# A second MLP product from seven quarter products, with work moved between VectorE, ScalarE and GpSimd around it

## The chip, the cores and the metric

The kernel runs on one core of one Trainium2 chip, in one launch. The metric is the device time in microseconds, as the median of several executions. An engine-by-engine profile of one execution stands beside it. The engines go by these names: PE is TensorE (PEld is its loading of stationary operands), DVE is VectorE, ACT is ScalarE, POOL is GpSimd, and SP is the engine that issues most of the DMAs.

## The reference

The input x has the shape (4, 64, 512, 64). Everything is float32. The output has 4 × 4096 tokens of width 256. Cut to what matters:

```
h = rfft_patches(x) @ W.T                        # tokens of width 256
y = layernorm(h)                                 # z of the kernel
r = y + retention(layernorm(y))                  # q * scan(decay, k * v)
a = relu(layernorm(r) @ W1.T + b1)               # 256 -> 1024
h = h + r + a @ W2.T + b2                        # 1024 -> 256, "second MLP product"
t = layernorm(h)                                 # tok of the kernel
h = h + t + sum over the two best experts e of weight_e * (gelu(t @ w1[e] + b1[e]) @ w2[e] + b2[e])
```

## The kernel before

The 16384 tokens are worked on in 32 blocks of 512 tokens (four tiles of 128). The loop over blocks is a software pipeline: in one iteration `new` (block i) is embedded, normed and sent through retention, `mid` (block i−1) goes through the MLP, and `old` (block i−2) is routed to its experts. Beside that, tiles of 256 tokens that already wait in a buffer in device memory (`xbuf`, sorted by expert) go through their expert in "slots" (`slot`, which calls `expert_step`), four in an iteration once the pipeline is full. The loop has 31 iterations; the work of the last block, and what is then left of the two before it, is written out by hand behind it.

The order of work on SP, PE, DVE and ACT is the order in which the program issues it (`manual_schedule`); each of these engines works strictly down its list. GpSimd is not in that list: its order is chosen by the framework's scheduler, from what is ready and from the order in the program. Within one iteration the order is this:

1. `embed` (L337 to L386): ten products of `xv` and `wu` on PE (L353; forty instructions), which DVE adds up into `h` (L359, L379); two norm factors by GpSimd (`factors`, L243 to L248); DVE then writes `zz`, the norm of the norm, and `z`, the first norm's result (L252 in `Norm.apply`). Between the first two parts `features2` of mid joins the turned halves to `hT` on ACT, and `rows`, `turn3` and `store` of old are issued. Ahead of the last part comes `sum_up` of mid (L462, L463): h + z + b2 on DVE.
2. A slot. Then eight `mlp_in(m)` of mid: a product on PE (L298) and a ReLU on ACT (L482), which frees a PSUM buffer; there are four such buffers (`p_mm`). After m = 1 stands `split1`: from block 6 on, two ACT copies (L278, `planes`) and a DMA that turns them; in blocks 0 to 5 PE turns `zz` instead. After m = 3 stands a slot. After m = 5 come `differences` of the next block (nine DVE instructions, L327 and L330) and `features1`, which joins the turned halves to `hT` on DVE (L292).
3. `logits` of old on PE (L557), `retention(0)` and `retention(1)` of new (three products each; ACT L416; DVE L418, L426, L436), with `choose` of old (sixteen small DVE instructions, L579 to L595) between them. `place` (PE L624, DVE L626 to L635) gives every row its place in `xbuf`; `take` (L702 to L744) works out a table of the tiles that have become full, in small DVE instructions on one partition. GpSimd writes the rows into `xbuf` by eight indirect DMAs (`scatter`, L647).
4. A slot, `mlp_out(0)`, `residual` (PE L451, DVE L454; then `factors_here` on DVE and `zz`), a slot, `split2`, the loads of the next tiles, and `mlp_out(1)`.

`mlp_out(u)` multiplies two tiles of 128 tokens, 8 × 2 products of 128 × 128 with 128 × 256 (L492; every float32 product is two instructions), and adds them to `h` (L499). After the second call come the norm statistics, the factor on GpSimd, `tok` (L252 again) and `by`.

A slot issues, in this order: the load of a tile (`load`: weights `w`, transposing read `xh`, and `xg`, all on SP, with the table's values read into registers), `turn` (ACT L806), `enter` (PE L813, ACT gelu L821), `leave` (PE L830), and `sums` (DVE L842 to L849, then two indirect DMAs of GpSimd that add into the output, L853).

Of the kernel before, what the change touches and what calls it, by code (L numbers as in the profile page):

```python
# [19 lines left out]
P = 128  # L20
# [15 lines left out]
def vit_tower_kernel(  # L36
# [21 lines left out]
    KD, KH = D // P, H // P  # L58
    J = STRIDE // 2
# [90 lines left out]
    w2_sb = const.tile([P, KH, D], F32)  # L150
    nc.sync.dma_start(out=w2_sb, in_=w2.rearrange("(k p) d -> p k d", p=P))
# [14 lines left out]
    nc.gpsimd.iota(tile_f, pattern=[[1, KMAX]], base=0, channel_multiplier=0, allow_small_or_imprecise_dtypes=True)  # L166
    ones_e = const.tile([1, E], F32)
# [24 lines left out]
    six = ctx.enter_context(tc.tile_pool(name="six", bufs=6))  # L192
# [116 lines left out]
    class Block:  # L309
# [5 lines left out]
        def differences(self, xb):  # L315
# [22 lines left out]
            more(v[0], v[0], 2.0, v[3])  # L338
            less(v[4], s0[:, :, 1:], s2)
            more(v[4], v[3], -2.0, v[4])  # L340

        def embed(self):
# [40 lines left out]
            self.z = one.tile([P, TT, D], F32, name="z")  # L383
            self.zz = one.tile([P, TT, D], F32, name="zz")
            norm.apply(self.zz, self.h, 1)
            norm.apply(self.z, self.h, 0)  # L386
# [74 lines left out]
        def sum_up(self):  # L461
            nc.vector.tensor_tensor(self.h, self.h, self.z, ALU.add)  # L462
            nc.vector.tensor_tensor(self.h, self.h, mb2_sb.unsqueeze(1).to_broadcast([P, TT, D]), ALU.add)  # L463
# [19 lines left out]

        def mlp_out(self, u, between=None):
            if u == 0:
                self.norm = Norm()
            ps = p_tm.tile([P, 2, D], F32, name="tm")
            for i in range(2):
                if i and between:
                    between()  # L490
                for k in range(KH):
                    last_product[0] = nc.tensor.matmul(  # L492
                        ps[:, i, :],
                        lhsT=self.aT[:, k, ts(u * 2 + i, P)],
                        rhs=w2_sb[:, k, :],
                        start=k == 0,
                        stop=k == KH - 1,
                    )
            nc.vector.tensor_tensor(self.h[:, ts(u, 2), :], ps, self.h[:, ts(u, 2), :], ALU.add)  # L499
            for i in range(2):  # L500
                self.norm.stats(self.h, u * 2 + i)
            if u == U - 1:
                self.norm.factors_here() if self.i >= NS - 1 else self.norm.factors()
                self.tok = one.tile([P, TT, D], F32, name="tok")
                self.norm.apply(self.tok, self.h)
                if self.i == NS:
                    nc.vector.tensor_tensor(self.h, self.h, self.tok, ALU.add)
                    return
                mean, rstd = self.norm.mv[:, :, 0], self.norm.rstd[:, 0, :]
                self.by = small.tile([P, 2, TT], F32, name="by")  # L510
                nc.vector.tensor_scalar(self.by[:, 0, :], rstd, 1.0, None, ALU.add)
                nc.vector.scalar_tensor_tensor(self.by[:, 1, :], mean, -1.0, rstd, ALU.mult, ALU.mult)
# [52 lines left out]
        def choose(self):  # L565
# [7 lines left out]
            lg = small.tile(shape, F32, name="lg")  # L573
# [8 lines left out]
            key = small.tile(shape, F32, name="key")  # L582
            self.oh = oh = small.tile([P, 2, TT, E], F32, name="oh")
# [35 lines left out]
        def place(self, at_once=True):  # L619
# [5 lines left out]
            before = small.tile([P, TT, E], F32, name="before")  # L625
# [70 lines left out]
    def take(n, block, writes):  # L696
# [17 lines left out]

# [24 lines left out]
        if block.i >= NS - 1:  # L739
            nc.vector.tensor_scalar(table[:, 2, :], table_f[:, 0, :], float(E - 1), None, ALU.min)  # L740
# [9 lines left out]
    def load_bank():  # L750
# [4 lines left out]
        for e in range(E):  # L755
            nc.scalar.dma_start(out=bank[0][:, e, :], in_=wex[ts(e, P), :])
            loaded.append(e)
            yield

    AHEAD = 4  # L760
    last_product = [None]
    tiles = []
    added = []
# [448 lines left out]
```

## Time and profile before

| What | Value |
|---|---|
| Median of 3 runs (lowest to highest) | 2172.19 us (2169.8 to 2180.58) |
| Profiled execution | 2177.78 us, span 2176.0 us |
| PE busy | 2149.1 us, 99% |
| DVE busy | 1648.2 us, 76% |
| ACT busy | 831.3 us, 38% |
| POOL busy | 874.5 us, 40% |
| Second MLP product (L492) on PE | 453.5 us, 2048 instructions |
| Mean granted PE clock | 0.993 |

A group's row in the profile reads: line, engine, operation, what is written from what, shapes, count; then the time in which the group was busy and the mean length of one instruction in ns; then the time that the engine idled just before the group, and on what. PE's instructions overlap, so the mean length is longer than the time from one start to the next. A line of the timeline reads: start in us, length, engine, line, operation, operands, count of merged instructions, and in brackets the idle time before and what ended it. Lengths on POOL are rough.

### The profile page before, as it was taken

The page shows a single profiled execution, that of the slowest core. Times are in us where ns is not written, and L with a number is a line of the kernel's source. Part 1 is how long each engine was busy: PE and PEld are TensorE (multiplying, and loading weights), DVE is VectorE, ACT ScalarE, POOL GpSimd, SP SyncE. Part 2 cuts the span into 40 slices and gives each one's busy share as a digit, 9 for nine tenths or more (in the row PEclk, how much of TensorE's full clock was granted, in tenths as well). Part 3 has the DMA queues.
Part 4 walks back from the last instruction along what each step waited for, and adds up shares of the span by engine and source line. Part 5 has one row for each costly group of instructions (what it writes and reads, how often), then busy time and mean ns, then how long its engine had stood idle before and what let it go on. Part 6 is the DMA issues. An engine that isn't in the chain of part 4 may idle for free.

```text
span 2176.0 us, 28966 instructions
## 1 busy us (share of the span) xinstructions
PE 2149.1 (99%) x8548; PEld 1546.0 (71%) x8548; DVE 1648.2 (76%) x5150; ACT 831.3 (38%) x1329; POOL 874.5 (40%) x760
## 2 busy tenths in 40 slices
PE   8999999999999999999999999999999999998999
PEld 6666666677776667777666777666777766676776
DVE  6678877778778778777877877877787887766454
ACT  1222333444334444433444443344343334442543
POOL 1022233444443344444334444433444443355444
PEclk9999999999999999999999999999999999999999
DMA  3032255765666776565677655576755666788743
GB/s 137 20 98 76 76 129 127 161 146 127 136 127 148 151 161 142 132 134 128 148 151 161 141 133 123 130 150 152 166 121 131 137 133 152 135 166 219 118 67 46
DMA packets 425390, 284.96 MB, mean 131 GB/s; under 512 B 355216, under 2 KB 391056, under 8 KB 421136
## 3 DMA queue, kind: packets, MB, share of 16 engines
q1 hardware_dynamic: 374304, 210.21, 42.0%
q0 software_dynamic: 49632, 67.39, 17.3%
q10 hardware_dynamic: 1296, 5.52, 0.9%
q8 instruction: 67, 1.10, 0.2%
q14 instruction: 91, 0.75, 0.1%
HBM read 118.36 MB, written 88.39 MB: 95 GB/s over the span
## 4 chain that ended last, share of the span: by engine, by line
PE 93%; DVE 3%; DMA 2%; issue 1%; another core or an unknown queue 0%; ACT 0%; DVEq 0%; SPq 0%
PE mm L298 33%; PE tm L492 19%; PE tm L353 13%; PE mm L813 10%; PE tm L830 10%; DMA turned<-planes 2%; PE sm L557 2%; PE tm L905 1%; PE mm L888 1%; PE tm L451 1%; PE mm L131 1%; PE mm L265 1%; PE sm L624 0%; DVE ks L426 0%; PE sm L204 0%
## 5 line engine op out<-in xcount | busy, mean ns | idle before, releaser
L853 POOL DMA_INDIRECT out<-y,xg x262 | 428.2, 1634 | 468.5 <-DVE y L849 210.2
L298 PE MATMUL mm<-hT,w_sb 128*128 128x512 f32 x1024 | 452.1, 594 | 4.3 <-issue 4.3
L492 PE MATMUL tm<-w_sb,aT 128*128 128x256 f32 x2048 | 453.5, 379 | 1.7 <-DVE h L499 1.7
L492 PEld LDWEIGHTS tm<-w_sb,aT 128*128 128x128 f32 x2048 | 388.6, 190 | 55.8 <-DVE h L499 2.1
L298 PEld LDWEIGHTS mm<-hT,w_sb 128*128 128x128 f32 x1024 | 194.6, 191 | 222.1 <-issue 213.2
L647 POOL DMA_INDIRECT xbuf<-row,to x248 | 243.7, 983 | 259.1 <-DVE full L708 182.6
L298 PE MATMUL mm<-hT,wqkv_sb 128*128 128x512 f32 x768 | 342.5, 602 | 2.3 <-DVE hT L292 2.2
L353 PE MATMUL tm<-wu,xv 128*128 128x256 f32 x1280 | 284.8, 381 | 0.0
L298 PEld LDWEIGHTS mm<-hT,wqkv_sb 128*128 128x128 f32 x768 | 145.2, 192 | 174.6 <-issue 159.0
L353 PEld LDWEIGHTS tm<-wu,xv 128*128 128x128 f32 x1280 | 244.2, 191 | 33.3
L821 ACT ACTIVATE ge<-mm,w 128x256 f32<-128x256 f32 x262 | 109.2, 468 | 405.7 <-issue 356.0
L813 PE MATMUL mm<-xT,w 128*128 128x256 f32 x1048 | 250.8, 382 | 0.0
L482 ACT ACTIVATE aT<-mm,vec 128x512 f32<-128x512 f32 x256 | 172.6, 684 | 204.7 <-PE mm L298 202.7
L830 PE MATMUL tm<-w,ge 128*128 128x256 f32 x1048 | 248.8, 380 | 0.9 <-DVE y L847 0.9
L830 PEld LDWEIGHTS tm<-w,ge 128*128 128x128 f32 x1048 | 200.0, 191 | 31.8 <-issue 3.4
L813 PEld LDWEIGHTS mm<-xT,w 128*128 128x128 f32 x1048 | 194.8, 190 | 37.0 <-issue 14.1
L806 ACT COPY xT<-xh 128x512 uint16<-128x512 uint16 x262 | 181.3, 762 | 11.3 <-DMA xh<-xbuf 6.3
L243 POOL TENSOR_SCALAR rstd<-mv 128x4 f32<-128x4 f32 x62 | 41.6, 672 | 317.2 <-DVE mv L224 315.3
L278 ACT COPY planes<-zz 128x1024 uint16<-128x1024 uint16 x100 | 99.6, 1043 | 163.9 <-issue 101.5
L847 DVE TENSOR_TENSOR y<-tm,w 128x512 f32<-128x512 f32 x131 | 90.6, 692 | 69.0 <-PE tm L830 65.2
L416 ACT ACTIVATE ks<-mm,vec 128x512 f32<-128x512 f32 x64 | 44.0, 687 | 243.2 <-PE mm L298 243.2
L597 POOL TENSOR_TENSOR ex<-euler,second 128x4 f32<-128x4 f32 x32 | 34.5, 1079 | 240.7 <-DVE second L589 240.7
(155 smaller groups left out, 2445.2 us busy)
## 6 DMA issues: line engine op xcount, KB each, us to landing
w<-in_wex SPq DMA_DIRECT2D x113, 641.5 KB
xb<-in_x SPq DMA_DIRECT2D x32, 1040.0 KB
out<-h SPq DMA_DIRECT2D x31, 512.0 KB
bank<-in_wex ACTq DMA_DIRECT2D x8, 641.5 KB
out<-y,xg POOLq DMA_INDIRECT x262
xbuf<-row,to POOLq DMA_INDIRECT x248
xh<-xbuf SPq DMA_TRANSPOSE x131
xg<-xbuf SPq DMA_DIRECT2D x131, 4.0 KB
```

The source lines that it names most:

```text
L278: nc.scalar.copy(planes[:, :, i * D : (i + 1) * D], half)
L298: nc.tensor.matmul(ps, lhsT=w[:, k, ts(m, P)], rhs=rhs[:, k, :], start=k == 0, stop=k == KD - 1)
L353: nc.tensor.matmul(ps[:, n, :], lhsT=xv[:, i, j, :], rhs=wu[:, i, j, :], start=j == 0, stop=j == J - 1)
L482: nc.scalar.activation(self.aT[:, m, :], ps, AF.Relu, bias=vec[:, MB1 + m : MB1 + m + 1])
L492: last_product[0] = nc.tensor.matmul(ps[:, i, :], lhsT=self.aT[:, k, ts(u * 2 + i, P)], rhs=w2_sb[:, k, :], start=k == 0, stop=k == KH - 1,)
L647: write = nc.gpsimd.indirect_dma_start(out=xbuf, out_offset=bass.IndirectOffsetOnAxis(ap=self.to[:, c, t : t + 1], axis=0), in_=self.row[: ...
L806: nc.scalar.copy(halves[:, :, :, 1 - i], self.xh[:, i * KD : (i + 1) * KD, :])
L813: nc.tensor.matmul(ps[:, m, :], lhsT=self.w[:, k * D + m * P : k * D + (m + 1) * P], rhs=self.xT[:, k, :], start=k == 0, stop=k == KD - 1,)
L821: nc.scalar.activation(self.ge[:, m, :], ps[:, m, :], AF.Gelu, bias=self.w[:, 5 * D + m : 5 * D + m + 1])
L830: last_product[0] = nc.tensor.matmul(ps[:, c, :], lhsT=self.ge[:, k, ts(c, P)], rhs=w[:, (2 + k) * D : (3 + k) * D], start=k == 0, stop=k ...
L847: nc.vector.tensor_tensor(y, ps, w[:, 4 * D : 5 * D].unsqueeze(1).to_broadcast([P, 2, D]), ALU.add)
L853: add = nc.gpsimd.indirect_dma_start(out=out, out_offset=bass.IndirectOffsetOnAxis(ap=self.xg[:, c, NUMBER - D : NUMBER - D + 1], axis=0), ...
```

## The change

The second MLP product is written as a product of 2 × 2 blocks by Strassen's method (in Winograd's form). The left operand, the 512 × 1024 activations, and the right one, 1024 × 256 weights, are cut into quarters; seven products of quarters replace the eight. The weight combinations are made once (`combine_weights`), those of the activations in each block on DVE (`combine1`, `combine2`), and the products are added into `h` by DVE; `mlp_out` now has three calls (16, 32 and 64 instructions of width 128).

Beside it, work moves. `sum_up` goes from DVE to GpSimd, and is issued later. The first norm's `z` goes from DVE to ACT (`result1`). `take`'s second half goes from DVE to GpSimd, up to block 27, in simpler instructions. `differences` is split in two. The slot ahead of `mlp_in` no longer issues a load; the load comes after `split1`, whose transposes so stand ahead of it on SP; `store` comes after m = 4. `xh` has four buffers in place of six, and some small tiles one in place of two. S1, S2 and S4 use the buffers of `tok`, `tokT` and `kv`. The diff, cut:

```diff
-    w2_sb = const.tile([P, KH, D], F32)
-    nc.sync.dma_start(out=w2_sb, in_=w2.rearrange("(k p) d -> p k d", p=P))
+    w2_sb = const.tile([P, 7, KQ, P], F32)
+    w2_raw = w2.rearrange("(r k p) (c d) -> p r c k d", p=P, k=KQ, d=P)
+    for i, (r, c) in {B11: (0, 0), B21: (1, 0), B22: (1, 1), T1: (0, 1)}.items():
+        nc.sync.dma_start(out=w2_sb[:, i], in_=w2_raw[:, r, c])
+    def combine_weights():
+        nc.vector.tensor_tensor(w2_sb[:, T3], w2_sb[:, B22], w2_sb[:, T1], ALU.subtract)
+        nc.vector.tensor_tensor(w2_sb[:, T1], w2_sb[:, T1], w2_sb[:, B11], ALU.subtract)
+        nc.vector.tensor_tensor(w2_sb[:, T2], w2_sb[:, B22], w2_sb[:, T1], ALU.subtract)
+        nc.vector.tensor_tensor(w2_sb[:, T4], w2_sb[:, B21], w2_sb[:, T2], ALU.subtract)
...
-            self.z = one.tile([P, TT, D], F32, name="z")
...
-            norm.apply(self.z, self.h, 0)
+            self.norm1 = norm
+        def result1(self):
+            mean, rstd = self.norm1.mv[:, :, 0], self.norm1.rstd[:, 0, :]
+            less = small.tile([P, TT], F32, name="less")
+            self.z = one.tile([P, TT, D], F32, name="z")
+            nc.vector.scalar_tensor_tensor(less, mean, -1.0, rstd, ALU.mult, ALU.mult)
+            for t in range(TT):
+                nc.scalar.activation(
+                    self.z[:, t, :],
+                    self.h[:, t, :],
...
-        def sum_up(self):
...
+        def sum_up(self, engine=nc.gpsimd):
+            engine.tensor_tensor(self.h, self.h, self.z, ALU.add)
+            engine.tensor_tensor(self.h, self.h, mb2_sb.unsqueeze(1).to_broadcast([P, TT, D]), ALU.add)
...
+        def combine1(self):
+            self.A11, self.A12 = [self.aT[:, i * KQ : (i + 1) * KQ, : BLK // 2] for i in range(2)]
+            self.A21, self.A22 = [self.aT[:, i * KQ : (i + 1) * KQ, BLK // 2 :] for i in range(2)]
+            shape = [P, KQ, BLK // 2]
+            self.S1 = one.tile(shape, F32, name="tok")
+            self.S2 = one.tile(shape, F32, name="tokT")
+            self.S3 = self.A21
+            nc.vector.tensor_tensor(self.S1, self.A21, self.A22, ALU.add)
+            nc.vector.tensor_tensor(self.S2, self.S1, self.A11, ALU.subtract)
+            nc.vector.tensor_tensor(self.S3, self.A11, self.A21, ALU.subtract)
+        def combine2(self, place):
+            self.S4 = one.tile([P, KQ, BLK // 2], F32, name=place)
+            nc.vector.tensor_tensor(self.S4, self.A12, self.S2, ALU.subtract)
         def mlp_out(self, u, between=None):
+            def product(to, a, b):
+                for i in range(2):
+                    for k in range(KQ):
+                        last_product[0] = nc.tensor.matmul(
+                            to[:, i, :],
+                            lhsT=a[:, k, ts(i, P)],
+                            rhs=w2_sb[:, b, k, :],
...
+            def add(to, what):
+                nc.vector.tensor_tensor(to, to, what, ALU.add)
+            h = self.h.rearrange("p (a i) (c d) -> p a c i d", i=2, d=P)
+            U = self.aT[:, 0, : BLK // 2].rearrange("p (i d) -> p i d", d=P)
             if u == 0:
...
+                self.ps = p_sm.tile([P, 2, 2, P], F32, name="sm")
+                product(self.ps[:, 0], self.A11, B11)
+                nc.scalar.copy(U, self.ps[:, 0])
+                add(h[:, 0, 0], U)
+                return
+            if u == 1:
+                ps = p_tm.tile([P, 2, 2, P], F32, name="tm")
+                product(ps[:, 0], self.A12, B21)
...
+                product(ps[:, 1], self.A22, T4)
+                add(h[:, :, 0], ps)
+                return
+            product(self.ps[:, 1], self.S2, T2)
+            product(self.ps[:, 0], self.S1, T1)
+            add(U, self.ps[:, 1])
+            add(h[:, 0, 1], U)
+            add(h[:, :, 1], self.ps[:, 0].unsqueeze(1).to_broadcast([P, 2, 2, P]))
...
+            product(ps[:, 0], self.S3, T3)
+            product(ps[:, 1], self.S4, B22)
+            add(U, ps[:, 0])
+            add(h[:, 1], U.unsqueeze(1).to_broadcast([P, 2, 2, P]))
+            add(h[:, 0, 1], ps[:, 1])
+            self.norm = Norm()
+            for t in (2, 3, 0, 1):
+                self.norm.stats(self.h, t)
...
+        engine = nc.vector if block.i >= SOON else nc.gpsimd
...
+    SOON = NS - 3
...
-            self.xh = six.tile([P, 2 * KD, S], U16, name="xh")
+            self.xh = four.tile([P, 2 * KD, S], U16, name="xh")
...
-    def slot(known):
+    def slot(known, load=True):
...
-                old.store()
             next(embed)
             next(embed)
-            if mid:
-                mid.sum_up()
+            if i + 1 < NB:
+                blocks[i + 1].differences(xs.pop(i + 1), 0)
             next(embed, None)
-            slot(known)
+            slot(known, load=False)
...
                     new.split1()
+                    if at["enter"]:
+                        advance("load", at["enter"] + AHEAD - 1)
                 if m == TT - 1:
                     slot(known)
+                if m == KH // 2 and old:
+                    old.store()
                 if m == KH - 3:
-                    blocks[i + 1].differences(xs.pop(i + 1))
+                    blocks[i + 1].differences(None, 1)
                     new.features1()
+                    if mid:
+                        mid.sum_up()
...
+            if mid:
+                mid.combine1()
             for m in range(KD):
                 new.retention(m)
+                if m == 0:
+                    new.result1()
                 if old and m == 0:
                     old.choose()
...
             slot(known)
+            if mid:
+                mid.mlp_out(0)
             if old:
                 old.scatter(2, last_product[0])
             if mid:
-                mid.mlp_out(0)
+                mid.combine2("kv")
+                mid.mlp_out(1)
             if old:
                 old.scatter(3, last_product[0])
             new.residual()
-            slot(known)
+            slot(known, load=False)
...
             if mid:
-                mid.mlp_out(1)
+                mid.mlp_out(2)
```

In `take`, the instructions from `base` (L716) to `taken` (L744) go to `engine`. The two sums over experts (L730, L732), which reduced along the row, become halving adds, and instructions with three operands become two, so that fourteen instructions become seventeen.

## The prediction

> **What bounds the kernel now.** I read the page first, then TensorE's timeline of one steady block (number 15 of 32, 1005 to 1069 us), then the same stretch of GpSimd, VectorE and ScalarE, then the waits.
>
> From the page:
>
> ```profile
> PE 2149.1 (99%) x8548; PEld 1546.0 (71%) x8548; DVE 1648.2 (76%) x5150; ACT 831.3 (38%) x1329; POOL 874.5 (40%) x760
> L492 PE MATMUL tm<-w_sb,aT 128*128 128x256 f32 x2048 | 453.5, 379 | 1.7 <-DVE h L499 1.7
> ```
>
> TensorE never rests, and the product that changes (L492) takes 453.5 us of it, with 1.7 us of waiting. Timeline of TensorE (start, length, count):
>
> ```profile
> 1009.68 7.07 PE L492 MATMUL tm<-w_sb,aT 128*128 128x256 f32 x32
> 1016.59 1.04 PE L451 MATMUL tm<-ident,ret 128*128 128x128 f32 x8
> ...
> 1020.92 7.07 PE L492 MATMUL tm<-w_sb,aT 128*128 128x256 f32 x32
> 1027.82 8.80 PE L353 MATMUL tm<-wu,xv 128*128 128x256 f32 x40
> ...
> 1050.23 7.03 PE L298 MATMUL mm<-hT,w_sb 128*128 128x512 f32 x16
> 1057.10 1.85 PE L557 MATMUL sm<-rw_sb,tokT 128*128 128x8 f32 x16
> 1058.80 10.55 PE L298 MATMUL mm<-hT,wqkv_sb 128*128 128x512 f32 x24
> ```
>
> Work follows work without a gap, so a stall anywhere lengthens the block. A 256-wide instruction takes 6.91/32 = 216 ns from start to start. GpSimd in the same block:
>
> ```profile
> 1011.60 1.06 POOL L647 DMA_INDIRECT xbuf<-row,to  x1 [6.46 <-DVE full L708]
> ...
> 1024.39 0.96 POOL L647 DMA_INDIRECT xbuf<-row,to  x1 [0.30 <-issue]
> 1028.04 1.61 POOL L853 DMA_INDIRECT out<-y,xg  x1 [2.69 <-DVE y L849]
> 1029.95 1.57 POOL L853 DMA_INDIRECT out<-y,xg  x1 [0.30 <-DVE mv L224]
> 1031.59 0.23 POOL L243 TENSOR_SCALAR rstd<-mv 128x4 f32<-128x4 f32 x1
> 1031.91 1.04 POOL L248 TENSOR_TENSOR rstd<-rstd,mhalf 128x4 f32<-128x4 f32 x1
> ...
> 1039.65 1.11 POOL L243 TENSOR_SCALAR rstd<-mv 128x4 f32<-128x4 f32 x1 [6.58 <-DVE mv L224]
> ```
>
> GpSimd is only 40% busy, but from 1011.6 on it is a queue: eight scatters (1.28 us apart), four scatter-adds (1.9 apart), and behind them the norm's factor (L243, L248), for which VectorE waits. VectorE and ScalarE after it, and the wait in total:
>
> ```profile
> 1032.99 1.38 DVE L252 TENSOR_SCALAR tok<-h,mv,rstd 128x256 f32<-128x256 f32 x4 [3.06 <-POOL rstd L248]
> 1039.48 1.19 DVE L462 TENSOR_TENSOR h<-h,z 128x1024 f32<-128x1024 f32 x1
> ...
> 1043.77 1.38 DVE L252 TENSOR_SCALAR zz<-h,mv,rstd 128x256 f32<-128x256 f32 x4 [1.84 <-POOL rstd L248]
> ```
>
> ```profile
> 1045.24 1.99 ACT L278 COPY planes<-zz 128x1024 uint16<-128x1024 uint16 x2 [1.01 <-DVE zz L252]
> 1047.14 1.26 ACT L482 ACTIVATE aT<-mm,vec 128x512 f32<-128x512 f32 x2
> ```
>
> ```profile
> DVE tok L252 <- POOL rstd L248: 81.2, 30, 3.1
> ```
>
> This is the chain that TensorE would meet next: factor, tok, VectorE's work on the new embedding, zz, planes, and behind planes the ReLUs that free PSUM.
>
> [...] the 8-wide logits (L557), each with a load, take (1058.80 − 1057.10)/16 = 106 ns, and single ones start 112 ns apart. [...] L243 took 0.23 us with VectorE idle and 1.11 beside L462. [...]
>
> **The change, part by part, per block.**
>
> *Products.* Out: 64 instructions at 216 ns = 13.8 us. In: 7 products × 2 × 4 × 2 passes = 112 of width 128. Their multiplying alone would be half of 216, 108 ns (the 128-wide transposes, L451, do 8 in 0.87 us, 109 each), so the load's 112 decides: 12.5. Gain 1.3 us × 32 = 41. Bounds: at 106 ns 1.9 per block (62 us); if loads did not overlap, 190 ns (L492's own load row on the weight-load engine), 21.3 us and 240 lost; the logits exclude that. I take 41.
>
> *VectorE.* In: four combinations of 1024 elements at 1.2 (L462) = 4.8; five adds of 256 at 0.4 and three of 512 at 0.69 (L499) = 4.1 in place of 1.4; one small factor 0.2. Out: residual sums 2.4 (L462, L463), first norm's z 1.4, fourteen instructions of the table (L716 to L744, 1011.85 to 1014.3) 2.45. Net +1.4, or 45 us on 1648: not a bound by sum. The three first combinations lie between the last ReLU (1058.0) and the first value product (1062.6, where VectorE idles 3.4 us): 3.6 fits into 4.6, cost nothing; without that cover, up to 3.6. The small factor stands ahead of choose, whose result the placing product awaits with 0.4 to spare: 0.2 × 29 = 5 us.
>
> *ScalarE.* z costs 2.07 (as L518) and a copy of 256 some 0.4: +80 us on 831, covered by the 4.5 us in which it waits for L298; without it, 2 us on the next ks.
>
> *Transfers.* split1's transposes were issued at 1051.23 though planes ended at 1047.23, because the queue held a tile's load (1046.76 to 1050.63). Now the load's three DMAs and two register loads come after them, and a store of 512 KB after mlp_in 4. That is up to 4 us for hT, which gates retention at 1058.80. Loads run three tiles ahead, so theirs cost nothing; nor do four xh buffers and the single ones, freed a step or a block earlier.
>
> *GpSimd.* Seventeen table instructions per block, chained. Each at least 0.32 us (L243 to L248), at most 0.67 (L243's mean, waits included): 5.4 to 11.4; I take 0.38[...]: 6.5. In program order they stand ahead of scatter, scatter-adds and factor. Two residual sums: [...] at least VectorE's 1.2. They are ready once z is, and behind what stands earlier.
>
> *Where that goes.* Let E be the end of the second product, 1027.8 before and 1026.5 after. Before, tok starts at E + 5.2. After: GpSimd's queue 1011.6 + 17.8 + 6.5 = 1035.9, factor 1.4: 1037.3, E + 10.8. VectorE is ready earlier: three last adds 1.5 and four statistics at 0.6, E + 4.1. How late may tok be? zz followed tok's start by 10.8 + 1.3 = 12.1 before; after, six difference instructions at 0.6 replace sums and idling, about the same. Planes take 2.0, the third ReLU 0.7, latencies 0.3; TensorE needs that PSUM buffer at its sixth mlp_in, 1050.23 + 1.72 = E + 24.1. So zz by E + 21.1, tok by E + 9.0. (hT's way, zz + 2.1 + 5.5 for the transpose, 1028.46 to 1034.01, + 1.5 to E + 31.0, allows 0.8 more.) Late by 1.8. The residual sums follow the factor on GpSimd, just where VectorE wants two-input adds on the embedding; held 0 to 2.8 us, I take 1.0. Stall: 2.8 us per block.
>
> It holds only from block 6 on, where zz is turned by planes: 25 blocks, 70 us. Sum: −41 + 70 + 5, and 2 to 3 in the tail, where TensorE has one expert step (3.45) over four combinations (4.8) and the longer last adds: +37. The profiled execution took 2177.8 (span 2176.0), 0.3% over the median 2172.2; so 2215 against it, **2209** against the median. At start, three more issues (about 1 us each) and four weight combinations (2.8) lie in block 0, where VectorE waits.
>
> **Rivals.**
> *A, faster.* GpSimd absorbs it: table instructions near 0.32, sums in its idle stretch (1059.3 to 1067.5), tok in time. Then −41 + 5 + 3: **2139**. It decides where the stall is below 33/25 = 1.3 us, that is, added GpSimd time ahead of tok plus VectorE's hold below 6.1 (I have 7.5). For it: the margin is thin, and 40% busy leaves room. Against: that queue already ran 1.7 us behind the statistics.
> *B, much slower.* The scheduler, which orders GpSimd by readiness, puts the sums ahead of the factor: 4.4 more, stall 6.2, 155 us: 2172 − 41 + 155 + 8 = **2294**. For it: z is ready some 10 us before the factor. Against: the queue still holds earlier work then.
> *C, slower elsewhere.* The sums run near 1059, beside the combinations: VectorE held up to 4.4, 1.0 of it covered, so about 2.5 on kv, choose and the placing product: −41 + 29 × 2.5 + 8: **2211**.
>
> **How the numbers follow.** Forecast 0.35 (own range 2183 to 2245), A 0.32 (2125 to 2161), C 0.13, B 0.12, all but cancelling 0.08. The forecast and C give one time by one cause, GpSimd's new work holding VectorE, and carry it over A. Within 0.5% (2161 to 2183; a measurement can hardly tell less from no change) falls 0.10; below 0.32; above 0.58. Below 2130 lies 0.06 of A, above 2265 most of B: range 2130 to 2265.
>
> **What would show it.** Right: width-128 products start 112 ns apart; VectorE's wait at tok grows from 2.7 us each to 7 or more; TensorE shows gaps of 2 to 3 us at mlp_in or retention. A: the wait at tok stays under 6 and TensorE shows none. B: the two sums stand ahead of L243's successor. C: gaps at the placing product. The forecast is wrong if the table's instructions take under 0.3 us, if scatters overlap them, or if loads and 128-wide products interfere (over 112 ns, slower whatever GpSimd does).

## The result and the profile after

The changed kernel takes **2275.41 us** (median of 4 runs, 2274.43 to 2277.9) against 2173.43 us for the kernel before in the same comparison. The ratio is 1.0467, with a 95% interval of [1.0438, 1.0496]. The forecast was 2209, in a range of 2130 to 2265: the sign was right, but the loss is 102 us and not 37.

The profiled execution took 2276.34 us, with a span of 2274.6 us. Its busy times, and the rows of the new product and of the MLP's first product (columns as in the profile before):

```profile
PE 2139.8 (94%) x10084; PEld 1560.7 (69%) x10084; DVE 1781.5 (78%) x4949; ACT 895.0 (39%) x1489; POOL 1140.1 (50%) x1280
...
L543 PE MATMUL tm<-w_sb,aT 128*128 128x128 f32 x1536 | 184.2, 277 | 0.0
...
L312 PE MATMUL mm<-hT,w_sb 128*128 128x512 f32 x1024 | 470.4, 604 | 91.6 <-ACT ge L912 44.4 <-ACT aT L518 43.0 <-issue 4.0
```

PE is busy for 9 us less than before, but it is busy for only 94% of the span. The product is as fast as forecast: its instructions start 112 ns apart, so that it takes 12.5 us of a block where it took 13.8. The loss is in another product, `mlp_in` (L312): 91.6 us of waiting, half on the gelu of an expert tile (`ge`), half on the third ReLU (`aT`). One steady block in PE's timeline:

```profile
1018.52 8.80 PE L375 MATMUL tm<-wu,xv 128*128 128x256 f32 x40
...
1030.61 5.31 PE L312 MATMUL mm<-hT,w_sb 128*128 128x512 f32 x12
1037.65 1.98 PE L312 MATMUL mm<-hT,w_sb 128*128 128x512 f32 x4 [1.73 <-ACT ge L912]
...
1046.63 5.42 PE L312 MATMUL mm<-hT,w_sb 128*128 128x512 f32 x12 [1.83 <-ACT aT L518]
```

The second product ends at 1018.5, which is the E of the prediction. The fourth `mlp_in` starts 1.7 us late and the sixth 1.8. GpSimd in the same block shows why, and VectorE and ScalarE show what hangs on it:

```profile
1018.42 0.97 POOL L731 DMA_INDIRECT xbuf<-row,to  x1 [0.30 <-issue]
1019.41 2.36 POOL L498 TENSOR_TENSOR h<-h,z 128x1024 f32<-128x1024 f32 x1
1021.85 2.70 POOL L499 TENSOR_TENSOR h<-h,mb_sb 128x1024 f32<-128x1024 f32 x1
1024.70 0.99 POOL L731 DMA_INDIRECT xbuf<-row,to  x1 [0.15 <-issue]
...
1030.82 0.23 POOL L257 TENSOR_SCALAR rstd<-mv 128x4 f32<-128x4 f32 x1
```

```profile
1019.17 3.16 DVE L552 TENSOR_TENSOR h<-h,aT 128x512 f32<-128x512 f32 x1
1022.25 0.41 DVE L552 TENSOR_TENSOR h<-h,tm 128x256 f32<-128x256 f32 x1
1022.58 0.41 DVE L237 BATCH_NORM_STATS2 st<-h 128x6 f32<-128x256 f32 x1
...
1024.61 0.18 DVE L238 BATCH_NORM_AGGREGATE mv<-st 128x2 f32<-128x6 f32 x1
1032.21 1.38 DVE L266 TENSOR_SCALAR tok<-h,mv,rstd 128x256 f32<-128x256 f32 x4 [7.41 <-POOL rstd L262]
```

```profile
1033.63 1.99 ACT L617 COPY row<-tok 128x1024 uint16<-128x1024 uint16 x2 [6.45 <-DVE tok L266]
1035.53 1.38 ACT L897 COPY xT<-xh 128x512 uint16<-128x512 uint16 x2
1036.77 0.82 ACT L912 ACTIVATE ge<-mm,w 128x256 f32<-128x256 f32 x2
...
1044.00 1.99 ACT L292 COPY planes<-zz 128x1024 uint16<-128x1024 uint16 x2 [5.25 <-DVE zz L266]
1045.90 1.26 ACT L518 ACTIVATE aT<-mm,vec 128x512 f32<-128x512 f32 x2
```

The two residual sums (L498, L499) stand between two scatters, ahead of the norm's factor (L257). tok so starts at E + 13.7 (1032.21 − 1018.52), where it was E + 5.2 before. ScalarE, which works down its list, is held at `row` (which reads tok), so the gelu that frees a PSUM buffer is late; 10 us later it is held at `planes` (which read zz), so the third ReLU is late. VectorE does lose time beside the first sum: an addition (L552) takes 3.16 us instead of 0.69. But that is not what makes tok late here. Its last addition and the norm statistics run beside the second sum at their usual lengths, and the last statistic ends at 1024.79, 6.0 us before the factor starts; in blocks 7 to 30 that distance is 6.0 to 6.1 us throughout. In the changed kernel it is the place of the sums in GpSimd's queue that counts. In the whole run VectorE's wait at tok grew from 81.2 to 192.9 us:

```profile
DVE tok L266 <- POOL rstd L262: 192.9, 30, 7.4
```

The second loss is in the first blocks. I measure a block from its first embedding product to the next block's. Against the profiled execution of before, blocks 0 to 5 are 21.9 us longer in sum, blocks 6 to 30 are 73.7 us longer (2.9 each), and the last one with the tail is 2.5 us longer. In blocks 2 to 4 the new first product waits for its PSUM bank (`sm`), which VectorE still reads for `place`:

```profile
212.03 3.63 PE L543 MATMUL sm<-w_sb,aT 128*128 128x128 f32 x16 [3.47 <-DVE before L714]
```

It waits 3.5 us, and then its sixteen instructions take 3.6 us instead of 1.95, since they start some 213 ns apart: the granted clock is 0.5 from 212.2 to 215.6 us.

### The profile page after: what moved, and what is told of

The parts are those of the page before. It is cut to its first block, busy times and chain, and to the rows that moved or that the text cites. A ratio compares the mean times of both kernels' runs of the same rounds, so it can differ in the third digit from the quotient of the medians.

```text
span 2274.6 us, 32705 instructions
## 1 busy us (share of the span) xinstructions
PE 2139.8 (94%) x10084; PEld 1560.7 (69%) x10084; DVE 1781.5 (78%) x4949; ACT 895.0 (39%) x1489; POOL 1140.1 (50%) x1280
## 4 chain that ended last, share of the span: by engine, by line
PE 45%; DVE 25%; POOL 15%; issue 8%; ACT 4%; DMA 2%; SPq 1%; POOLq 0%; ACTq 0%; DVEq 0%
PE mm L312 21%; POOL xbuf L731 5%; PE tm L543 5%; POOL out L944 5%; PE mm L904 4%; DVE st L237 3%; PE tm L921 3%; PE sm L543 3%; POOL h L498 3%; PE sm L641 2%; DVE h L381 2%; DVE xv L348 2%; DVE zz L266 2%; PE tm L375 2%; DVE mv L238 2%
## 5 line engine op out<-in xcount | busy, mean ns | idle before, releaser
L944 POOL DMA_INDIRECT out<-y,xg x262 | 441.4, 1685 | 355.7 <-DVE y L940 133.3
L312 PE MATMUL mm<-hT,w_sb 128*128 128x512 f32 x1024 | 470.4, 604 | 91.6 <-ACT ge L912 44.4
L312 PEld LDWEIGHTS mm<-hT,w_sb 128*128 128x128 f32 x1024 | 191.4, 192 | 329.7 <-issue 188.0
L731 POOL DMA_INDIRECT xbuf<-row,to x248 | 253.3, 1021 | 252.9 <-DVE full L792 184.2
L312 PE MATMUL mm<-hT,wqkv_sb 128*128 128x512 f32 x768 | 338.4, 597 | 1.5 <-DVE hT L306 1.5
L312 PEld LDWEIGHTS mm<-hT,wqkv_sb 128*128 128x128 f32 x768 | 143.8, 191 | 170.7 <-issue 155.3
L266 DVE TENSOR_SCALAR tok<-h,mv,rstd 128x256 f32<-128x256 f32 x128 | 44.2, 409 | 193.0 <-POOL rstd L262 192.9
L897 ACT COPY xT<-xh 128x512 uint16<-128x512 uint16 x262 | 181.3, 760 | 10.6 <-DMA xh<-xbuf 10.6
L543 PE MATMUL tm<-w_sb,aT 128*128 128x128 f32 x1536 | 184.2, 277 | 0.0
L518 ACT ACTIVATE aT<-mm,vec 128x512 f32<-128x512 f32 x256 | 164.6, 689 | 44.1 <-PE mm L312 44.1
L543 PEld LDWEIGHTS tm<-w_sb,aT 128*128 128x128 f32 x1536 | 179.2, 194 | 0.1
L257 POOL TENSOR_SCALAR rstd<-mv 128x4 f32<-128x4 f32 x62 | 25.9, 417 | 265.2 <-DVE mv L238 263.4
L617 ACT COPY row<-tok 128x1024 uint16<-128x1024 uint16 x62 | 61.7, 1043 | 212.8 <-DVE tok L266 212.8
L416 ACT ACTIVATE z<-h,less,rstd 128x256 f32<-128x256 f32 x128 | 66.4, 588 | 150.4 <-DVE lg L663 132.4
```

Source lines behind the costliest of these rows:

```text
L266: nc.vector.tensor_scalar(dst[:, t, :D], src[:, t, :], self.mv[:, t, 0:1], self.rstd[:, i, t : t + 1], ALU.subtract, ALU.mult,)
L312: nc.tensor.matmul(ps, lhsT=w[:, k, ts(m, P)], rhs=rhs[:, k, :], start=k == 0, stop=k == KD - 1)
L518: nc.scalar.activation(self.aT[:, m, :], ps, AF.Relu, bias=vec[:, MB1 + m : MB1 + m + 1])
L543: last_product[0] = nc.tensor.matmul(to[:, i, :], lhsT=a[:, k, ts(i, P)], rhs=w2_sb[:, b, k, :], start=k == 0, stop=k == KQ - 1,)
L731: write = nc.gpsimd.indirect_dma_start(out=xbuf, out_offset=bass.IndirectOffsetOnAxis(ap=self.to[:, c, t : t + 1], axis=0), in_=self.row[: ...
L897: nc.scalar.copy(halves[:, :, :, 1 - i], self.xh[:, i * KD : (i + 1) * KD, :])
```

## The experiments

My theory after the result: the two sums on GpSimd cost on both sides. They lengthen the queue ahead of tok's factor by 5.1 us, and while they run they hold VectorE's instructions up. The rivals: that the queue alone counts (the table's seventeen instructions included), or that the seven products themselves are too much for VectorE. The table gives all runs: the median, the ratio to the kernel before measured beside it, and the lengths of the blocks against the profiled execution of before, added up as above.

| Run | Median, us | Ratio, 95% interval | Blocks 0–5 | Blocks 6–30 | Block 31 |
|---|---|---|---|---|---|
| changed kernel | 2275.41 | 1.0467 [1.0438, 1.0496] | +21.9 | +73.7 | +2.5 |
| a1: sums on VectorE | 2210.69 | 1.0167 [1.0144, 1.0190] | +12.8 | +15.0 | +4.6 |
| a2: table on VectorE | 2283.43 | 1.0496 [1.0467, 1.0524] | +27.4 | +77.0 | +3.1 |
| a3: sums behind the factor | 2280.40 | 1.0485 [1.0461, 1.0508] | +27.4 | +71.1 | +2.9 |
| a4: first products swapped | 2295.60 | 1.0556 [1.0521, 1.0591] | +12.1 | +101.9 | +3.5 |
| a5: tok's factor on VectorE | 2224.97 | 1.0246 [1.0226, 1.0265] | +23.5 | +12.6 | +3.0 |
| b1: sums on VectorE, ahead of the join | 2162.50 | 0.9957 [0.9942, 0.9971] | +10.2 | −30.0 | +3.1 |
| b2: seven products alone | 2227.31 | 1.0248 [1.0228, 1.0269] | +14.5 | +29.0 | +5.6 |
| b3: sums on GpSimd, in the kernel before | 2317.90 | 1.0662 [1.0637, 1.0688] | +11.8 | +130.2 | +3.7 |
| c1: b1 with its first blocks mended | 2148.02 | 0.9892 [0.9872, 0.9912] | −1.5 | −28.8 | +9.2 |
| c2: b1, table on VectorE | 2172.09 | 1.0008 [0.9994, 1.0022] | +2.1 | −9.6 | +0.7 |
| c3: b1, z on VectorE | 2198.14 | 1.0116 [1.0087, 1.0144] | +12.1 | +14.4 | +2.7 |
| c4: b1, transfers put back | 2205.46 | 1.0147 [1.0121, 1.0172] | +9.4 | +30.3 | +2.0 |

### The sums: on GpSimd or not, and where in its queue

**a1_sums_dve**, the changed kernel with the sums on VectorE, at the same place behind the join of `hT`:

```diff
-                        mid.sum_up()
+                        mid.sum_up(nc.vector)
```

> The kernel after, with the two residual sums back on VectorE at the place where the program issues them (behind the join of hT). Queue theory (what GpSimd does ahead of tok's factor sets tok, and tok sets the waits at mlp_in): 5.1 us leave GpSimd's queue, the wait at tok falls from 6.4 us to about 2 each, TensorE's waits at mlp_in (some 100 us) go; but VectorE gets 2.4 us just ahead of the three combinations, where it is just in time for kv, so up to 2.2 us per block come back at the placing product: 2200 to 2240. Rival (VectorE's own added work makes zz late): no better than the kernel after, 2275 or more.

2210.69 us: 65 us of the 102 go with one word. The waits for the gelu and the third ReLU at `mlp_in` are gone. The largest that is left is on VectorE, where the sums' 2.4 us now stand between the join and the combinations (waits of PE: total, times, longest):

```profile
PE sm L708 <- DVE both L679: 28.2, 24, 2.3
```

**a3_sums_behind**, the sums kept on GpSimd, but bound to follow the factor of the new block's norm:

```diff
+            self.made = nc.gpsimd.tensor_tensor(self.rstd, self.rstd, mhalf[:, 0:n, :], ALU.pow)
...
+            if behind is not None:
+                after(first, [behind])
...
-                        mid.sum_up()
+                        mid.sum_up(behind=new.norm1.made)
```

> The kernel after, with one order added: GpSimd's first residual sum of a block waits for the factor of the new block's embedding, so that the two sums stand behind both factors in place of among the scatters. No instruction moves to another engine. Queue theory: tok's factor comes 5.1 us earlier, the waits at mlp_in (4 us in each of 25 blocks) go: about 2175, less if the early blocks gain too. Rival (VectorE's own work, or the sums' hold on VectorE wherever they stand): 2260 to 2275.

2280.4 us, no gain. The queue did become shorter: tok starts at 1032.15 where E is 1023.44, that is E + 8.7, within the E + 9.0 that the prediction had allowed. But the sums now run beside zz. VectorE, and then GpSimd:

```profile
1042.48 5.51 DVE L266 TENSOR_SCALAR zz<-h,mv,rstd 128x256 f32<-128x256 f32 x4
```

```profile
1042.23 2.53 POOL L498 TENSOR_TENSOR h<-h,z 128x1024 f32<-128x1024 f32 x1
1044.84 2.35 POOL L501 TENSOR_TENSOR h<-h,mb_sb 128x1024 f32<-128x1024 f32 x1
```

zz took 5.51 us instead of 1.38, nearly the sums' whole length of 4.96 us. planes and the third ReLU are late again, and PE waits 3.0 us at `mlp_in`. A shorter queue alone thus buys nothing if the sums then stand beside zz: their second cost, the hold on VectorE, comes in where the first one went.

**a5_factor_dve**, the opposite cut: the sums stay in the queue, but tok no longer waits for it, since VectorE works out the factor:

```diff
-            self.norm.factors_here() if self.i >= NS - 1 else self.norm.factors()
+            self.norm.factors_here()
             self.tok = one.tile([P, TT, D], F32, name="tok")
```

> The changed kernel with tok's factor worked out on VectorE (factors_here) in every block, so that tok no longer waits for GpSimd's queue; the sums stay on GpSimd. If the queue ahead of the factor is the whole loss: the waits at mlp_in go, some 2180 to 2195 (VectorE gets a few small instructions more). If the hold of VectorE by the sums is what counts: zz or the additions for the embedding still take some 3 us longer beside them, and 2230 to 2265 is left.

2224.97 us, between the two expectations' ranges but near the second. With tok out of the queue (it starts at E + 8.7) the steady blocks lose 12.6 us in sum instead of 73.7, so the place in the queue is worth some 61 us in them. Against b1 below, which has the sums on VectorE, 43 us remain in these 25 blocks. They hold both VectorE's held addition (3.16 us, as in the changed kernel) and the factor's own small instructions there, which this run doesn't separate.

**b3_sums_in_before**, the kernel before with this one edit, the sums on GpSimd behind `features1` (the sums that are written out behind the loop stay on VectorE, as in the changed kernel):

```diff
-        def sum_up(self):
...
+        def sum_up(self, engine=nc.gpsimd):
...
-            if mid:
-                mid.sum_up()
             next(embed, None)
...
                     new.features1()
+                    if mid:
+                        mid.sum_up()
```

> The kernel before, with one edit: the two residual sums on GpSimd, issued behind features1. Theory (5 us of sums lengthen GpSimd's queue ahead of tok's factor and hold VectorE besides): a stall of 2 to 3.5 us per block, some 60 to 100 in all: 2235 to 2275. Rival (it takes the table and the combinations too to make the chain late): 2165 to 2190.

2317.9 us: 145 us lost, more than I expected, and without any of the new products or the table. VectorE's instructions beside the two sums, then GpSimd's sums:

```profile
953.73 3.08 DVE L231 TENSOR_SCALAR mv<-mv 128x4 f32<-128x4 f32 x1
...
958.67 2.96 DVE L236 SCALAR_TENSOR_TENSOR st<-st,mv 128x4 f32<-128x4 f32 x1
```

```profile
954.42 2.36 POOL L462 TENSOR_TENSOR h<-h,z 128x1024 f32<-128x1024 f32 x1
...
959.22 2.37 POOL L463 TENSOR_TENSOR h<-h,mb_sb 128x1024 f32<-128x1024 f32 x1
```

Two instructions on four columns, 0.17 us each elsewhere, took 3.08 and 2.96 us, and each ends about 0.04 us after a sum (956.81 against 956.78, 961.63 against 961.59). Behind them on VectorE's list stand the residual's zz, the expert sums (`y`) and the norm statistics, all late with them: in the middle one of the steady blocks the last statistic ends at E + 7.3, where it was E + 2.1 before. Here it is not the queue that makes tok late, since GpSimd itself stands idle for VectorE's `y`, ahead of the factor:

```profile
964.87 1.62 POOL L853 DMA_INDIRECT out<-y,xg  x1 [3.28 <-DVE y L849]
```

```profile
969.82 1.38 DVE L252 TENSOR_SCALAR tok<-h,mv,rstd 128x256 f32<-128x256 f32 x4 [3.16 <-POOL rstd L248]
```

tok starts at E + 10.6 (969.82 − 959.27), and the new block's zz, planes, `hT` and retention follow; PE waits at the embedding, at `mlp_in` and at retention. PE at retention:

```profile
995.15 7.25 PE L298 MATMUL mm<-hT,wqkv_sb 128*128 128x512 f32 x13 [1.78 <-DVE hT L292]
```

The wait is 1.78 us, but thirteen such instructions, which take 7.25 us here, take 5.7 at the pace of `mlp_in` in the same block (twelve in 5.31 us, 0.43 us from start to start): 1.5 us more are lost behind the wait. So this stall cost more than itself, as did the one of 3.47 us above.

### The table

**a2_table_dve**, the changed kernel with the table on VectorE:

```diff
-        engine = nc.vector if block.i >= SOON else nc.gpsimd
+        engine = nc.vector
```

> The kernel after, with all of the table's seventeen instructions on VectorE; the sums stay on GpSimd. Queue theory: 4.9 us leave GpSimd's queue ahead of tok's factor, tok starts near E + 7.5 in place of E + 12.4, the waits at mlp_in go, and VectorE takes 3.4 us more behind place, where it can still be late with sums: 2180 to 2200. Rival (VectorE's own work): VectorE has more to do, so 2275 or more.

2283.43 us, a miss for the theory of the queue. Without the table GpSimd is earlier, and the sums now run beside the residual's small norm instructions and its zz, which lose 2.9 and 2.8 us around 1157.9 us, where a block begins; the expert sums (`y`) stand behind zz. VectorE's zz, GpSimd's second sum, and PE's wait for `y` at the embedding:

```profile
1157.93 4.17 DVE L266 TENSOR_SCALAR zz<-z,mv,rstd 128x256 f32<-128x256 f32 x4
```

```profile
1158.92 2.38 POOL L499 TENSOR_TENSOR h<-h,mb_sb 128x1024 f32<-128x1024 f32 x1
```

```profile
PE tm L375 <- DVE y L938: 39.7, 25, 1.7
```

The gap moved, its size did not.

### The first blocks

**a4_swap**, `mlp_out(1)` ahead of `mlp_out(0)`, so that the first product doesn't need the bank that `place` holds:

```diff
-                mid.mlp_out(0)
+                mid.mlp_out(1)
...
-                mid.mlp_out(1)
+                mid.mlp_out(0)
```

> The kernel after, with the first two calls of mlp_out exchanged, so that the call that needs the bank of place comes second. My reading of the early blocks: without a slot between, the first product waits 3.6 us for VectorE to read place's bank, and the clock is lower for some 2 us after it, in blocks 2 to 4: 15 us less, about 2260; blocks with a slot gain at most 0.3 each, 2252. If the bank is not the cause: 2275.

2295.6 us, a miss on the whole. Blocks 2 and 3 did gain what was expected (+0.4 and −0.4 us against before, where they had +5.7 and +6.4), so the bank was their cause. But with the swap in all blocks GpSimd's order changed too: the whole table and two scatter-adds then stand ahead of six of the eight scatters, VectorE's wait at tok rose from 192.9 to 288.8 us, and the steady blocks lost 28 us more. So in this kernel the swap pays only in the first blocks, where no slots run beside it.

**b1_sums_ahead** takes both lessons: the sums on VectorE, ahead of the join of `hT`, where VectorE idled 2.2 us for the transposing DMA, and the swap in the first six iterations alone.

```diff
                     blocks[i + 1].differences(None, 1)
+                    if mid:
+                        mid.sum_up(nc.vector)
                     new.features1()
-                    if mid:
-                        mid.sum_up()
...
-                mid.mlp_out(0)
+                mid.mlp_out(1 if i < 6 else 0)
```

> The changed kernel with both residual sums on VectorE, put ahead of the join of hT (features1), where VectorE idles 2.2 us for the transposing DMA, and with mlp_out(1) before mlp_out(0) in the first six iterations alone. Theory (the sums cost by what they stand in front of, and the first product of the early blocks waits for the bank of place): the 1.6 us per steady block that were left with the sums behind the join go, 25 x 1.6 = 40 from 2211, and the early blocks give back some 10 to 15: 2155 to 2170, so faster than before. Rival (the combinations themselves are too late on VectorE, wherever the sums stand): the gap of about 1.2 us at the placing product stays, 2190 to 2205.

2162.5 us, ratio 0.9957 [0.9942, 0.9971]: faster than the kernel before by 0.4%, a small gain, but with the whole interval below 1. The steady block is 62.3 us, 1.1 less than before, close to the 1.3 of the product. Blocks 4 and 5 still lose 5.4 and 4.8 us. PE and ScalarE in block 4:

```profile
227.65 2.07 PE L312 MATMUL mm<-hT,w_sb 128*128 128x512 f32 x2 [5.06 <-ACT hT L280]
```

```profile
225.77 1.38 ACT L897 COPY xT<-xh 128x512 uint16<-128x512 uint16 x2 [8.62 <-DMA xh<-xbuf]
227.02 1.06 ACT L280 COPY hT<-mm 128x512 f32<-128x512 f32 x2
```

ScalarE waits 8.6 us for the first expert tile (`xh`), and the copies to `hT` stand behind it in its list. That tile's load was issued at 222.0 us; in the kernel before it was issued at 214.0. A load reads the table, and on GpSimd the table is late.

**c1_early_table** puts the table of blocks 0 to 4 back on VectorE; in block 0 it also leaves the differences whole and puts z behind the second retention:

```diff
-        engine = nc.vector if block.i >= SOON else nc.gpsimd
+        engine = nc.vector if block.i >= SOON or block.i < 5 else nc.gpsimd
...
-                if m == 0:
+                if m == (i == 0):
                     new.result1()
```

> b1_sums_ahead with the losses of its first blocks taken out: the table of blocks 0 to 4 on VectorE again (from block 4 on, the first tile's load came 8 us late, behind a table that GpSimd made late, and ScalarE's copies to hT stood behind that tile); in block 0 the differences whole and behind mlp_in, and z behind the second retention. Theory: blocks 4 and 5 were 5.4 and 4.9 us longer than in the kernel before and block 0 3.8; some 12 us of that go, from 2162.5 to 2147 to 2153. Rival (the first load is late for another reason, scatter or the queue): 2158 to 2164.

2148.02 us (2145.05 to 2157.35), ratio 0.9892 [0.9872, 0.9912], the fastest of all. The load is issued at 213.0, block 4 is 0.3 us longer than before instead of 5.4, block 0 not at all. Block 5 keeps 3.1. The profiled execution is one of the longer ones (span 2155.6): its tail holds a wait of 10.3 us for an expert tile that other profiled runs don't have.

### The product and the other moves, one at a time

**b2_product_alone**: the seven products without any of the moves: sums, z and table on VectorE, differences whole, loads and store at their old places.

```diff
                 old.turn3()
+                old.store()
...
+            if mid:
+                mid.sum_up(nc.vector)
             next(embed, None)
-            slot(known, load=False)
+            slot(known)
...
+            self.z = one.tile([P, TT, D], F32, name="z")
+            norm.apply(self.z, self.h, 0)
...
-        engine = nc.vector if block.i >= SOON else nc.gpsimd
+        engine = nc.vector
```

> The seven products alone: sums, first norm's z and table are on VectorE, differences whole, loads and store at the places they have in the kernel before; only the buffers are those of the changed kernel. Theory (the product gains 1.3 us per block and the loss comes from GpSimd's sums): -41 in the steady blocks, some +15 in blocks 0 to 5 (the bank of place) and +3 in the tail: 2145 to 2165. Rival (VectorE, which has the combinations, z, sums and table, is too late for TensorE, so the moves were needed): gaps at the placing product and at retention, 2185 to 2230.

2227.31 us, a miss for my theory: the seven products by themselves are slower by 2.5%, some 29 us of it in the steady blocks and 14.5 in the first, where the bank of `place` still counts. In steady blocks VectorE has become late in several places (waits of PE: total, times, longest):

```profile
PE mm L312 <- DVE hT L306: 12.1, 24, 1.2
PE tm L922 <- DVE h L553: 11.2, 23, 0.9
```

So the moves off VectorE were needed. Three runs take them away from b1 singly.

**c2_table_back** (table on VectorE), **c3_z_back** (z on VectorE, same place), **c4_transfers_back** (loads and store at their old places):

```diff
-        engine = nc.vector if block.i >= SOON else nc.gpsimd
+        engine = nc.vector
```

```diff
-            for t in range(TT):
-                nc.scalar.activation(
...
+            self.norm1.apply(self.z, self.h, 0)
```

```diff
-            slot(known, load=False)
+            slot(known)
...
-                if m == KH // 2 and old:
-                    old.store()
```

> b1_sums_ahead with the table on VectorE in all blocks. Theory (with four combinations and nine additions VectorE has no room for the table's 2.5 us between the placing product and the residual, as in the run with the product alone): gaps at the value products and the residual's transposes, about 1 us per steady block, less some 10 in the early blocks: 2172 to 2190. Rival (the table costs nothing there, GpSimd's 17 instructions were not worth it): 2145 to 2160.

> b1_sums_ahead with the first norm's result on VectorE instead of ScalarE, at the same place behind retention(0). Theory (it stands ahead of choose, whose result the placing product awaits with a few tenths of a us to spare): 1.4 less 0.2 us late, some 1 us in each of 29 blocks: 2180 to 2195. Rival (VectorE takes it in its idle time): 2160 to 2166.

> b1_sums_ahead with the loads and the store at the places that they have in the kernel before, so that the turning transposes stand behind a tile's load again. Theory (tok is later by GpSimd's table, so hT has no slack left): the join of hT waits up to 4 us longer, a gap at retention of 1 to 3 us in 25 blocks: 2185 to 2225. Rival (the transposes had the slack, as in the kernel before): 2160 to 2168.

All three are slower than b1, by their ratios 0.5, 1.6 and 1.9% (some 11, 35 and 41 us). c2 (2172.09) is at the lower edge of what the theory gave: it loses 20 us in the steady blocks and regains 8 in the first. c3 (2198.14) is a little over its range, c4 (2205.46) within it. The largest wait of PE in the steady blocks is that of the last expert product on VectorE's additions in c2 (10.6 us in 25 times), that of the placing product on `both` in c3 (18.8 in 29), and that of retention on the join of `hT` in c4:

```profile
PE mm L312 <- DVE hT L306: 23.8, 22, 2.4
```

Each wait is below 1.2 us on the mean, but with the smaller ones a steady block loses 0.8, 1.8 and 2.4 us (the differences to b1 in blocks 6 to 30, divided by 25). In c4 the mean granted clock is lower too: 0.973 in its profiled execution, against 0.989 in b1's (0.993 in c2's, 0.987 in c3's). These three moves each pay; the fourth, the sums on GpSimd, cost more than the product brought.

## Why the prediction was right and wrong

**The products: right.** 112 instructions, 112 ns apart, 12.5 us in place of 13.8; b1's steady blocks are 1.1 to 1.2 us shorter than before.

**The path: right for one of the two waits.** Factor, tok, zz, planes, third ReLU, sixth `mlp_in` is a chain that PE met, with 43.0 of the 91.6 us. From tok's start to zz's end were 12.1 us in the prediction and 11.7 in the trace. The allowed E + 9.0 was safe: in c1 tok starts at E + 9.1 (1024.68 − 1015.61) and no `mlp_in` of that block waits. It was also about 1 us too tight: with tok at E + 13.7 the two waits are 1.73 and 1.83 us, from which I estimate a limit near E + 10.1.

**GpSimd's queue: the step that failed.** The prediction has "The residual sums follow the factor on GpSimd". They run ahead of it and put their 5.1 us into the queue before it. The queue has three terms.
- *The table* was oversized. Seventeen instructions took some 5.0 us, not the 6.5 that an assumed 0.38 each had given (fourteen in 4.0, from 1006.1 to 1010.1, and three behind a scatter in 1.0). With the sums on VectorE, tok starts at E + 8.7 in the middle one of b1's steady blocks, and not at E + 10.8; 1.5 of these 2.1 us are this error. Without the sums in the queue there is no such stall at `mlp_in` (a1, b1).
- *The sums' place* was wrong. It was rival B's mechanism, at a chance of 0.12. Its argument against ("the queue still holds earlier work then") didn't hold, because the sums are ready while scatters are still to come, and the scheduler put them between these. Their length was nearly right: 2.36 and 2.66 us on the mean against 2.2 (half of rival B's 4.4), which was an assumption of mine: no row of before shows such a sum on GpSimd.
- *The hold on VectorE*, "0 to 2.8 us, I take 1.0", depends on the sums' place too. In the changed kernel it is 2.5 us, within these bounds, on one addition, and VectorE's wait for the factor covers it. Where the sums follow the factor, as the forecast had it, zz alone lost 4.1 us (a3), more than the bound, and the total was no better than with the wrong order; in the blocks shown of b3 and a2 VectorE lost 5.7 us. The 1.0 was an assumption of mine, which took the hold for a delay by chance; the case that it had from the trace of before is the other way round, GpSimd's L243 beside VectorE's L462. In the runs a held instruction lasts until the sum has ended, down to four columns (b3: its two end some 0.04 us after the sums). These two start 0.7 and 0.6 us before the recorded start of the sum, but lengths on POOL are rough, so what decides which instruction is held was not shown.

The stall that follows is 4.25 us per steady block (2.95 of loss and 1.3 of gain undone), where I had 2.8. It has a second place, which I had not seen: the row copies hold the gelu, and so the fourth `mlp_in`. By an estimate that place begins to count only from about E + 12 (13.7 less the wait of 1.7), so it is a consequence of the sums' place and no error at my E + 10.8.

**The first blocks: the second step that failed, since they were not in the sum.** "It holds only from block 6 on" left blocks 0 to 5 with the product's gain, some −8 us; they lost 21.9. The first product's bank (3.5 us in three blocks, and behind it starts 213 ns apart in place of 112, as in the block above) was charged nothing. "Loads run three tiles ahead, so theirs cost nothing" is false for the very first tile, whose load waits for the table (c1: 5 us in block 4). In block 0 the split differences and z on ScalarE delayed PE where the prediction had VectorE waiting (3.8 us, which c1 takes away).

**VectorE, ScalarE and the transfers.** The combinations do fit: in b1's block from 966 us on, PE has no recorded wait. But the sum has no term for what the other moves save, as if there were room without them, and c2 to c4 show that there was none: taking one away costs 11 to 41 us. The transfers' "up to 4 us for hT" were no spare but needed.

**The sum.** Forecast: −41 + 70 + 5 + 3. Measured by blocks: 73.7 in blocks 6 to 30 where the forecast has 42, 21.9 in blocks 0 to 5 where it has −8, 2.5 in the tail. About half of the miss is the sums' place, half the first blocks. Rival A's 2139 is what c1 nearly reaches (2148), by a route that A doesn't have: the sums not on GpSimd at all, and the first blocks mended.

## What to carry to other kernels

The two sums of 1024 columns were no free time on GpSimd here, though it had been only 40% busy. Price such sums twice: at their whole length in GpSimd's queue (here 5.1 us), ahead of whatever waits there, and at about their whole length on a VectorE instruction beside them that is held (here 2.5 us on an addition beside a sum of 2.36, 4.1 us on zz beside 4.96 us of sums in a3), and look at what has to finish then. When an engine's order is chosen by a scheduler, take as the likely case that a ready instruction is put ahead of the one that you care about. And price the first blocks of a pipeline by themselves: banks, first loads and lists that had slack in the steady state had none there, and blocks 0 to 5 lost 21.9 us.

## What was not expected of the hardware

- Beside a GpSimd sum of 1024 columns (2.36 and 2.66 us on the mean) some VectorE instructions lasted until it had ended, however small they were: 3.08 and 2.96 us for four columns in b3 (0.17 elsewhere), 3.16 us for a 512-wide addition of two SBUF operands in the changed kernel (0.69), 5.51 us for the four of zz beside both sums in a3 (1.38). Not all were held. In the changed kernel 104 norm statistics, 82 of their aggregates and 26 additions with one operand in PSUM ran beside the sums, and none was longer than usual (0.40, 0.18 and 0.41 us).
- PE ran at half its pace behind a wait. Behind the 3.47 us in the changed kernel sixteen instructions started some 213 ns apart in place of 112, at a granted clock of 0.5 from 212.2 to 215.6 us. In b3 a shorter wait, of 1.78 us, also had a slow stretch behind it: thirteen 512-wide instructions took 7.25 us in place of 5.7. Not every short wait has one: behind the waits of 1.73 and 1.83 us in the changed kernel's steady block the granted clock stays at 1.
- Chained GpSimd instructions on one partition and 1 to 32 columns mostly take 0.16 to 0.36 us from start to start (0.90 for the first one behind a scatter), 0.28 on the mean, against the 0.32 that I took for the least. A time under 0.3 us was one of the prediction's own signs of being wrong, and it came.
